# A cross-attention kernel on one core: a new hand-written order for the last ten tiles, and two weight splits moved in the head

## The chip, the cores and the metric

The kernel runs on one core of one Trainium2 chip. The metric is the device time of one execution in microseconds (us). Before the change the median of three runs is 506.95 us, the lowest 506.29 and the highest 507.17. The profile comes from one execution of its own.

## The reference

Queries come from x, keys and values from a context of 77 rows per batch, sixteen heads of 32; the output gets the residual x and a layer norm:

```python
qs = (q @ wq).reshape(Bq, Lq, H, HD).transpose(0, 2, 1, 3)
ks_ = (k @ wk).reshape(Bq, Lk, H, HD).transpose(0, 2, 1, 3)
vs = (v @ wv).reshape(Bq, Lk, H, HD).transpose(0, 2, 1, 3)
scores = jnp.einsum('bhqd,bhkd->bhqk', qs, ks_) / jnp.sqrt(jnp.float32(HD))
scores = jnp.where(mask[:, None, :, :], -jnp.inf, scores)
attn_w = jax.nn.softmax(scores, axis=-1)
attn = jnp.einsum('bhqk,bhkd->bhqd', attn_w, vs)
out = attn.transpose(0, 2, 1, 3).reshape(Bq, Lq, H * HD) @ wo + q
mu = jnp.mean(out, axis=-1, keepdims=True)
var = jnp.mean((out - mu) ** 2, axis=-1, keepdims=True)
return (out - mu) / jnp.sqrt(var + EPS) * gamma + beta
```

x is 4 x 2048 x 512 in fp32, the context 4 x 77 x 512 (both k and v), the mask 4 x 2048 x 77.

## The kernel before, in words

The 8192 rows of x are cut into 64 tiles of 128 rows, taken in 32 pairs; four tiles are a group of the query projection. The projections split each fp32 operand into a high and a low part and sum three products, so the query of a group (L192) and the output projection of a tile (L561) are twelve matmuls of 128x512 each per quarter or tile.

A tile goes through these steps. TensorE makes the scores (L321). VectorE takes each head's maximum and applies the mask (L364), ScalarE the exponential with its sum (L379), VectorE the reciprocal of the sums (L385), GpSimd the normalisation (L390), VectorE a transposition in 32x32 blocks into a buffer B (L413). For each pair of tiles twelve DMAs of 128 KB, the regroups (L425), put the blocks of B into a buffer PT with the keys on the partitions. TensorE multiplies PT with the values vsb (L459). ScalarE writes the high part of the result (L508), VectorE the low part (L512), and TensorE makes the output projection (L561). VectorE adds the rows of x, which a DMA of 256 KB has brought into an output buffer o (load L529, residual L564), and takes the statistics (L599, L606). The reciprocal root is GpSimd's (L638 or L634, then L639), the scaling ScalarE's (L585 or L648) or VectorE's (centre L669, finish L684), the affine step GpSimd's (L589, L590), and a DMA of 256 KB stores the tile (L593). There are eight buffers o; the last tiles use four `o_end` and four `o_last`, in space that other buffers leave.

The last tile, 63, is computed in other ways to finish sooner. Its probabilities are turned by TensorE and not by DMA (L439, L449), and its product needs the values with their rows in another order: `turn_values` (L615, L616) copies 19 and 58 rows of vsb, 2 KB each, into a spare buffer by two DMAs of SyncE. Tile 62 is finished in halves (L679 on ScalarE, L680 on GpSimd, L681), tile 63 by L664 and L674 on VectorE.

The order is written out by hand, and each engine runs its instructions in the order in which the program issues them. A head loop does tiles 0 to 5. A table PAIR of words is read once for each of the pairs 3 to 26. Then JOINT and ORDER, a table for the last ten tiles, are read once, word by word (`for word in (JOINT + ORDER).split(): do(*read(word))`, after L870). A word is a letter and a tile, pair or group piece, with a part behind the point:

- S scores, T maxima of four heads, e exponentials, r reciprocal, n normalisation, t transposition (tiles)
- P regroup of a pair, U regroup of one tile, V product with the values (pairs); a and b are the high and low part of its result, c and d the same for a tile
- O output projection, x load of x, + residual, s statistics, u reciprocal root, v bias, k scaling, p scaling on GpSimd, f affine step, y centre, z finish, B half a finish, w store
- Q query projection of a quarter group, q its evacuation, i and j the high and low part of x transposed
- R, E, X, W, h, m, I, J, M: the special steps of tiles 63 and others; Y0 is turn_values

A letter at the end of a P or U names the engine whose queue issues the DMA: s SyncE, g GpSimd, a ScalarE. Loads and stores are always issued by SyncE. A DMA that must wait (for a transposition, for a buffer that is to be emptied) holds all that stand behind it in its engine's list. The DMAs of SyncE signal on eight semaphores in rotation, so each also waits for the landing of the one eight places before it.

In the head loop, for u = 2, `split_wo` (L289) makes the low part of two of the four rows of the output weights on GpSimd, and `split_xT` (L180) the low part of x transposed.

Of the kernel before, what the change touches and what calls it, by code (L numbers as in the profile page):

```python
# [53 lines left out]
ORDER = """
S54 T54.3 i31 e54.3 T54.0 O49 q58 e54.0 k47 T54.2 T54.1 +49 t53 S55 T55.0 T55.1 Q59 f47 x50 x52 T55.3 e54.2 T55.2
e54.1 j31 r54 n54 O48 q59 s49 P26.9s +48 S56 e55.0 P26.4s e55.2 e55.1 e55.3 T56.1 T56.0 P26.6g P26.0s V25 T56.2 x51
r55 a25.0 a25.1 t54 e56.1 S57 e56.2 T56.3 T57.2 Q62 P26.2g P26.8s n55 e56.3 T57.1 Q60 t55 u49 b25.0 e56.0 P26.3g Q63
e57.1 p49 e57.2 T57.3 T57.0 r56 w47 s48 b25.1 P26.5s x59 e57.3 x53 S58 P26.10s P26.7g P27.7g q62 e57.0 k46 n56 q60
P27.0s q63 u48 p48 T58.1 T58.2 P26.1s P27.1s P26.11s T58.3 e58.1 r57 t56 P27.11s n57 Q61 P27.6s f46 e58.2 T58.0 V26
q61 a26.1 t57 a26.0 x55 f48 e58.0 S59 P27.2s T59.2 P27.5s e58.3 T59.3 e59.3 P27.3s P28.4g P27.8s T59.0 O51 b26.0  # L60
P28.11g T59.1 P27.9s +51 P28.6g r58 e59.2 P28.5g O50 P27.10s b26.1 s51 e59.1 P27.4s n58 S60 Y0 u51 +50 P28.0s x57
e59.0 P28.7g P28.10s V27 T60.0 T60.1 a27.0 T60.2 a27.1 T60.3 e60.1 r59 t58 w46 P28.3s P28.9s S61 n59 O52 P28.1s
e60.3 b27.0 s50 T61.0 T61.3 t59 f49 u50 e61.0 e61.3 T61.2 b27.1 T61.1 O53 P28.8s P29.1g P29.9g e61.2 O54 S62 +52
e61.1 +53 s52 x54 r61 P28.2s V28 +54 P29.7g e60.2 x62 T62.1 T62.2 O55 p50 n61 e60.0 T62.3 x56 P29.4s r60 n60 T62.0
t61 v51 M0 P29.8s a28.0 a28.1 b28.1 b28.0 f50 t60 +55 O57 e62.2 P29.6s e62.1 P29.5s P29.10s +57 P30.6g P29.3s
P29.11s k51 P29.2s P29.0s P30.10s P30.1s e62.0 e62.3 u52 v52 S63 V29 P30.2s T63.0 P30.9s P30.5g s53 P30.7g P30.11a
s55 T63.1 r62 a29.1 P30.4s T63.3 P30.0s e63.0 P30.3s n62 b29.1 T63.2 O56 a29.0 b29.0 e63.1 I54 u53 e63.3 P30.8s s57
h63.0 y55 t62 +56 f51 O59 u55 e63.2 x58 O58 x60 k52 m63.0 y54 V30 h63.1 m63.1 I56 U62.7s U62.6s +59 J56 a30.1 u56
U62.4s U62.8s R63.0 U62.9s x61 U62.11s s59 y57 a30.0 u57 +58 u59 b30.1 b30.0 U62.5s z57 R63.1 y53 J54 R63.3 U62.1s
U62.0a R63.2 w48 E63.0a f52 w51 s58 U62.10s O60 U62.3s y58 +60 w50 O61 U62.2a w52 X63 M1 z53 E63.1a v56 v59 s60 z55  # L70
+61 y60 E63.2a u54 W62 u58 k56 E63.3a w49 w57 u60 z54 k59 I61 c62 w54 J61 W63 f56 z58 c63 d62 y61 w53 z60 w55 u61
f59 O62 w56 d63 z61 +62 s62 y62 w58 w60 w61 w59 O63 u62 s63.0 s63.1 B62.0 u63 B62.1 y63 z63 w63
"""


# [1 line left out]
def xattn_layernorm(  # L77
# [100 lines left out]
    def split_xT(g, c):  # L178
        h, l = (a[:, c : c + 2] for a in gx[g])
        nc.gpsimd.tensor_tensor(l, fx[g, c], h.bitcast(F32), ALU.subtract)  # L180
# [107 lines left out]
    def split_wo(c):  # L288
        nc.gpsimd.tensor_tensor(wol[:, c], stage_b[:, 1, c], woh[:, c].bitcast(F32), ALU.subtract)  # L289
# [93 lines left out]
    def recip(t):  # L383
        ris[t] = sb.tile([P, H], F32, tag="ri", bufs=3, name=f"ri_{t}")
        nc.vector.reciprocal(ris[t], sums[t])  # L385
# [641 lines left out]
```

## Time and profile before

| what | value |
|---|---|
| median of 3 runs | 506.95 us (506.29 to 507.17) |
| the profiled execution | 506.36 us |
| its span, first to last instruction | 504.5 us |
| PE, DVE, ACT, POOL busy | 496.3, 462.7, 473.3, 428.2 us |
| regroups issued by SyncE, by GpSimd in the span | 355, 16 |

The profile is of one execution. PE is TensorE's matmuls and PEld its weight loads, which overlap; DVE is VectorE, ACT ScalarE, POOL GpSimd, SP SyncE. Busy times are sums over instructions of an engine that do not overlap in the sum. An arrow like `PT<-B` names what is written and read; `x12` counts. The queue rows (`SPq`) show when an engine issued a DMA and how long the issue took, not the transfer. Between the time of an execution and its span lie 1.86 us here. The chain of waits follows back from the last instruction what released each step. The table ORDER covers the time from about 414 us on.

### The profile page before, as it was taken

The numbers are of one execution on the slowest core, as the hardware profiler recorded it, in microseconds if no ns is written. First come the engines' busy times: TensorE is split into PE (matmuls) and PEld (weight loads), VectorE is DVE, ScalarE is ACT, GpSimd is POOL, SyncE is SP. The second block draws the span as 40 slices with busy tenths as digits, with TensorE's granted clock in tenths as the row PEclk, the third lists the DMA queues.
The fourth block names the chain that finished last, engine by engine and source line by source line (L and its number), as shares of the span: only waits on it lengthen the run. The fifth ranks groups of instructions, "written<-read, shape, count | busy, mean of one in ns | idle before, by whom it ended". The sixth has DMA issues, their size and how long they took to land.

```text
span 504.5 us, 20435 instructions
## 1 busy us (share of the span) xinstructions
PE 496.3 (98%) x6904; PEld 390.5 (77%) x6904; DVE 462.7 (92%) x2567; ACT 473.3 (94%) x2241; POOL 428.2 (85%) x385
## 2 busy tenths in 40 slices
PE   9999999999999999999999999999999999999995
PEld 7987778877777887777788777778877777777774
DVE  6698999999989988999999988999998889999997
ACT  6798999999999999999999999999999999999871
POOL 0659368989988998998999888899999888999996
PEclk9999999999999999999999999999999999999999
DMA  8945977677777789777778868978787888667665
GB/s 312 400 161 142 220 199 203 201 201 203 214 226 221 210 216 231 217 214 224 217 218 219 241 173 221 253 208 234 220 208 185 236 233 241 167 187 220 168 210 209
DMA packets 58424, 109.50 MB, mean 217 GB/s; under 512 B 9219, under 2 KB 11011, under 8 KB 58320
## 3 DMA queue, kind: packets, MB, share of 16 engines
q1 hardware_dynamic: 55920, 103.35, 72.6%
q0 software_dynamic: 1872, 4.20, 2.8%
q8 instruction: 55, 0.90, 0.8%
q10 hardware_dynamic: 528, 0.66, 0.4%
q14 instruction: 49, 0.40, 0.2%
HBM read 41.68 MB, written 16.78 MB: 116 GB/s over the span
## 4 chain that ended last, share of the span: by engine, by line
PE 82%; DVE 8%; ACT 5%; DMA 1%; POOL 1%; issue 1%; SPq 1%; DVEq 0%; POOLq 0%; ACTq 0%
PE pq L192 28%; PE po L561 26%; PE pa L459 10%; PE sc L321 6%; ACT pbuf L379 4%; PE sc L561 2%; PE sc_e L321 2%; DVE pbuf L364 2%; DVE B L413 2%; PE pv L258 2%; PE pk L218 1%; PE pq L729 1%; PE pq L190 1%; PE sc_f L321 1%; DVE AL L512 1%
## 5 line engine op out<-in xcount | busy, mean ns | idle before, releaser
L379 ACT ACTIVATE pbuf<-pbuf,nm 128x77 f32<-128x77 f32 x1024 | 352.5, 348 | 8.2 <-DVE nm L364 7.5
L379 ACT ACTIVATION_READ_ACCUMULATOR pbuf<-pbuf,nm 128x1 f32 x1024 | 193.1, 189 | 0.0
L390 POOL TENSOR_TENSOR pbuf<-pbuf,ri 128x1232 f32<-128x1232 f32 x63 | 145.8, 2316 | 19.8 <-DVE ri L385 11.8
L364 DVE CUSTOM_DVE_ANT_0 pbuf<-sc,mb 128x77 f32<-128x77 f32 x828 | 143.8, 231 | 5.9 <-PE sc L321 5.6
L192 PE MATMUL pq<-xtl,wqh 128*128 128x512 f32 (+1 forms) x256 | 98.3, 384 | 0.0
L192 PE MATMUL pq<-xth,wql 128*128 128x512 f32 (+1 forms) x256 | 98.2, 384 | 0.0
L413 DVE STREAM_TRANSPOSE B<-pbuf 128x1280 f32<-128x1280 f32 x63 | 94.6, 1502 | 0.5 <-POOL pbuf L390 0.2
L561 PE MATMUL po<-woh,AH 128*128 128x512 f32 x224 | 90.5, 404 | 0.0
L192 PE MATMUL pq<-xth,wqh 128*128 128x512 f32 (+1 forms) x230 | 88.6, 385 | 0.0
L561 PE MATMUL po<-wol,AH 128*128 128x512 f32 x224 | 87.3, 390 | 0.0
L561 PE MATMUL po<-woh,AL 128*128 128x512 f32 x224 | 86.5, 390 | 0.0
L589 POOL TENSOR_TENSOR o<-o,gam 128x512 f32<-128x512 f32 x53 | 68.7, 1297 | 20.8 <-ACT o L585 20.8
L364 DVE DVE_READ_ACCUMULATOR2_ANT nm<- 128x1 f32 x1024 | 84.2, 82 | 0.0
L590 POOL TENSOR_TENSOR o<-o,bet 128x512 f32<-128x512 f32 x53 | 68.4, 1291 | 4.2
L180 POOL TENSOR_TENSOR xtl<-xtf,xth 128x1024 fp32r<-128x1024 f32 x28 | 67.4, 2409 | 0.1
L459 PE MATMUL pa<-PT,vsb 96*32 96x256 f32 x960 | 58.2, 382 | 0.7 <-DVE ri L385 0.3
L321 PE MATMUL sc<-kct,q 32*64 32x77 f32 x3312 | 55.5, 239 | 0.4 <-DVE q L209 0.3
L192 PEld LDWEIGHTS pq<-xth,wql 128*128 128x128 f32 x256 | 48.2, 188 | 8.4
L192 PEld LDWEIGHTS pq<-xtl,wqh 128*128 128x128 f32 x256 | 48.1, 188 | 8.5
L321 PEld LDWEIGHTS sc<-kct,q 32*64 32x64 f32 x3312 | 48.8, 130 | 6.5 <-issue 5.1
L561 PEld LDWEIGHTS po<-woh,AH 128*128 128x128 f32 x224 | 42.0, 187 | 10.7 <-DVE nm L364 0.4
L192 PEld LDWEIGHTS pq<-xth,wqh 128*128 128x128 f32 x230 | 43.2, 188 | 8.9
(195 smaller groups left out, 852.8 us busy)
## 6 DMA issues: line engine op xcount, KB each, us to landing
PT<-B SPq DMA_DIRECT2D x355, 128.0 KB
xtf<-xT SPq DMA_DIRECT2D x28, 512.0 KB
o<-x SPq DMA_DIRECT2D x56, 256.0 KB
out<-o SPq DMA_DIRECT2D x56, 256.0 KB
PT<-B POOLq DMA_DIRECT2D x16, 128.0 KB, 4.4
xtf<-xT SPq DMA_DIRECT2D x4, 256.0 KB
stage_a<-wk SPq DMA_DIRECT2D x4, 256.0 KB
stage_b<-wv SPq DMA_DIRECT2D x4, 256.0 KB
```

The source lines that it names most:

```text
L180: nc.gpsimd.tensor_tensor(l, fx[g, c], h.bitcast(F32), ALU.subtract)
L192: nc.tensor.matmul(pq, wc, r[:, c, rs], start=(n == 0), stop=(n == 11))
L258: nc.tensor.matmul(pv, ctx_s[c][i][:, r, :], v[c], start=(n == 0), stop=(n == 11))
L321: nc.tensor.matmul(scs[t][g, j][r0 : r0 + n], qd[t // 4][q, g, at : at + n], kct[q, g, t // TPB, keys_of(j)], start=True, stop=True,)
L364: nc.vector.tensor_tensor_reduce(pb[:, i // 2, (i % 2) * NK : (i % 2 + 1) * NK], scs[t][g, j], mb[:, t % TPB, keys_of(h)], -1.0, CEIL, ALU ...
L379: nc.scalar.activation(p, p, AF.Exp, bias=nmax[t][:, i : i + 1], scale=-1.0, accum_out=sums[t][:, i : i + 1])
L390: nc.gpsimd.tensor_tensor(pv, pv, rv.to_broadcast((P, NP, 2, NK)), ALU.mult)
L413: nc.vector.transpose(bt.rearrange("p c q r -> p q c r"), pbuf[t % NPB].rearrange("p q (c r) -> p q c r", c=5),)
L459: nc.tensor.matmul(pas[b, g // 2][HD * j : HD * (j + 1), (g % 2) * BLK : (g % 2 + 1) * BLK], vsb[:, 2 * b // TPB, HD * h : HD * (h + 1)], ...
L561: nc.tensor.matmul(pos[t], a[:, c, rs], w[:, c], start=(first and n == 0), stop=(n == 11))
L589: nc.gpsimd.tensor_tensor(o, o, gam, ALU.mult)
L590: nc.gpsimd.tensor_tensor(o, o, bet, ALU.add)
```

## The change

Three edits. First, ORDER is replaced by a new order of the same words, for all engines; only the queues of the regroups differ: 16 were issued by GpSimd and are 8 now, 3 by ScalarE and are 2, and SyncE issues the other nine. Among the order's changes, the product V26 stands ahead of the scores S60 (before, ahead of S59), V25 ahead of S56 (before, behind it) and V28 ahead of S62 (before, behind it). Second, in the head loop at u = 2 the two `split_wo` go behind the two `split_xT`. Third, two unused entries come into the table of operations, which shift the lines behind L831 by one.

```diff
@@ ORDER (first and last lines of each)
-S54 T54.3 i31 e54.3 T54.0 O49 q58 e54.0 k47 T54.2 T54.1 +49 t53 S55 T55.0 T55.1 Q59 f47 x50 x52 T55.3 e54.2 T55.2
...
-f59 O62 w56 d63 z61 +62 s62 y62 w58 w60 w61 w59 O63 u62 s63.0 s63.1 B62.0 u63 B62.1 y63 z63 w63
+k47 i31 f47 j31 k46 S54 T54.0 e54.0 T54.2 e54.2 T54.3 q58 T54.1 O48 +48 t53 P26.9s P26.7s P26.2g P26.3s P26.1s P26.5s
...
+w52 w59 w61 w54 s62 O63 s63.0 y62 u62 B62.1 B62.0 s63.1 u63 y63 z63
@@ -785,8 +785,6 @@
         if u == 2:
             recip(1)
             normalise(1)
-            split_wo(0)
-            split_wo(1)
         for q in evac:
             q_evac(*q)
@@ -795,6 +793,9 @@
         for q in pieces(u):
             split_xT(*q)
+        if u == 2:
+            split_wo(0)
+            split_wo(1)
         if u == 0:
@@ -889,7 +890,7 @@
-        "v": bias_one, "K": stretch, "G": shift, "p": pool_scale, "I": act_mean, "J": act_squares, "M": keep,
+        "A": scores_pair, "D": scores_rest, "v": bias_one, "K": stretch, "G": shift, "p": pool_scale, "I": act_mean, "J": act_squares, "M": keep,
```

SyncE, at the head of the table, before the change (o_7713 is the load x50, o_7715 x52, o_7845 x51; PT_7755 belongs to pair 26 and out<-o_7226 is w47):

```order
L593 DMA out<-o_6928 128x512
L529 DMA o_7713<-x 128x512
L529 DMA o_7715<-x 128x512
L425 DMA PT_7755<-B_7559 32x2x512 x3
L529 DMA o_7845<-x 128x512
L425 DMA PT_7755<-B_7559 32x2x512
L593 DMA out<-o_7226 128x512
```

and, further on, before the change around turn_values (PT_8044 belongs to pair 27, PT_8198 to pair 28, out<-o_7197 is w46):

```order
L529 DMA o_8133<-x 128x512
L425 DMA PT_8044<-B_7853 32x2x512 x7
L615 DMA spare<-vsb 19x512
L616 DMA spare<-vsb 58x512
L425 DMA PT_8198<-B_8080 32x2x512
L529 DMA o_end<-x 128x512
L425 DMA PT_8198<-B_8080 32x2x512
L593 DMA out<-o_7197 128x512
```

The same place of SyncE after the change (PT_7974 is pair 27's, PT_8261 pair 28's; o_8164 is x51, o_8265 x54, o_8268 x50):

```order
L425 DMA PT_7974<-B_7873 32x2x512 x2
L529 DMA o_8164<-x 128x512
L593 DMA out<-o_7226 128x512
L615 DMA spare<-vsb 19x512
L616 DMA spare<-vsb 58x512
L425 DMA PT_7974<-B_7873 32x2x512 x4
L425 DMA PT_8261<-B_8065 32x2x512 x2
L529 DMA o_8265<-x 128x512
L425 DMA PT_8261<-B_8065 32x2x512
L529 DMA o_8268<-x 128x512
L425 DMA PT_8261<-B_8065 32x2x512 x3
```

The loads x50 and x52 have left the head of the table; turn_values stands ahead of four regroups of pair 27 and of x50, which is the eleventh DMA counted from L615.

SyncE after the change, around x52 (o_8626; PT_8462 is pair 29's, out<-o_7469 is w48, out<-o_7197 w46):

```order
L425 DMA PT_8462<-B_8289 32x2x512 x7
L593 DMA out<-o_7469 128x512
L425 DMA PT_8462<-B_8289 32x2x512
L593 DMA out<-o_7197 128x512
L425 DMA PT_8462<-B_8289 32x2x512
L529 DMA o_8626<-x 128x512
```

x52 now follows the regroups of pair 29, and it takes the buffer that w48 stores.

GpSimd's last instructions before the change (mvt_9043 is tile 62's statistics, mvt_9080 tile 63's):

```order
L638 TENSOR_TENSOR mvt_9043<-mvt_9043,small 128x1
L639 TENSOR_TENSOR mvt_9043<-mvt_9043,small 128x1
L680 TENSOR_TENSOR o_last<-o_last,bet 128x256
L639 TENSOR_TENSOR mvt_9080<-mvt_9080,small 128x1
L680 TENSOR_TENSOR o_last<-o_last,bet 128x256
```

and after it (mvt_9054 is tile 62's, mvt_9093 tile 63's):

```order
L589 TENSOR_TENSOR o_end<-o_end,gam 128x512
L590 TENSOR_TENSOR o_end<-o_end,bet 128x512
L638 TENSOR_TENSOR mvt_9054<-mvt_9054,small 128x1
L639 TENSOR_TENSOR mvt_9054<-mvt_9054,small 128x1
L680 TENSOR_TENSOR o_last<-o_last,bet 128x256 x2
L639 TENSOR_TENSOR mvt_9093<-mvt_9093,small 128x1
```

Tile 63's reciprocal root (the last L639) stood between the two halves of tile 62 and stands behind both.

More of the change, by code (lines that the diff above doesn't have):

```diff
@@ L54 @@
 ORDER = """
-S54 T54.3 i31 e54.3 T54.0 O49 q58 e54.0 k47 T54.2 T54.1 +49 t53 S55 T55.0 T55.1 Q59 f47 x50 x52 T55.3 e54.2 T55.2
[L56 to L69, printed above, removed]
@@ L70 @@
-U62.0a R63.2 w48 E63.0a f52 w51 s58 U62.10s O60 U62.3s y58 +60 w50 O61 U62.2a w52 X63 M1 z53 E63.1a v56 v59 s60 z55
-+61 y60 E63.2a u54 W62 u58 k56 E63.3a w49 w57 u60 z54 k59 I61 c62 w54 J61 W63 f56 z58 c63 d62 y61 w53 z60 w55 u61
-f59 O62 w56 d63 z61 +62 s62 y62 w58 w60 w61 w59 O63 u62 s63.0 s63.1 B62.0 u63 B62.1 y63 z63 w63
+k47 i31 f47 j31 k46 S54 T54.0 e54.0 T54.2 e54.2 T54.3 q58 T54.1 O48 +48 t53 P26.9s P26.7s P26.2g P26.3s P26.1s P26.5s
+P26.4s P26.11s Q59 s48 u48 q59 S55 T55.1 V25 e54.1 e54.3 a25.0 e55.1 T55.0 r54 e55.0 T55.2 T55.3 e55.3 e55.2 a25.1 S56
@@ new lines @@
+T56.1 T56.2 b25.0 T56.0 T56.3 e56.3 e56.1 e56.0 e56.2 n54 O49 +49 t54 P26.6s r55 Q60 S57 s49 T57.0 T57.3 T57.1 e57.0
+e57.1 Q61 q60 n55 P26.10g P26.0s p48 t55 P27.7s P26.8s S58 r56 T57.2 e57.3 e57.2 P27.11s P27.1s P27.2g u49 n56 p49
+b25.1 T58.1 T58.3 T58.2 e58.1 T58.0 e58.0 e58.2 t56 q61 Q62 Q63 r57 q62 S59 T59.0 T59.1 O51 x62 P27.4s P27.6s x60
+P27.5s P27.9s x51 w47 Y0 P27.10s P27.0s P27.3s V26 e58.3 e59.0 T59.3 T59.2 e59.3 q63 S60 n57 t57 P27.8s f48 +51 r58
+n58 f49 P28.4s P28.8s P28.7g x54 P28.9s x50 P28.3s P28.2s P28.1s T60.0 T60.2 T60.3 T60.1 t58 O50 a26.1 b26.1 e59.2
@@ new lines @@
+e59.1 +50 V27 a27.0 a27.1 b27.0 r59 n59 f46 e60.0 S61 T61.0 T61.1 e61.1 b27.1 T61.3 O54 s51 +54 O55 u51 a26.0 e61.3
+T61.2 e61.2 e61.0 s50 t59 x59 P28.6s P29.1g x55 P28.5s +55 x57 P28.10s P29.8g P28.11s x58 P28.0s x53 P29.4s P29.0s
+P29.2s u50 P29.9g P29.6s P29.5s P29.3s V28 S62 r61 b26.0 a28.0 a28.1 b28.1 b28.0 T62.1 T62.0 s55 T62.3 O57 n61 t61
+e60.1 e60.2 e60.3 r60 v51 p50 O52 +57 T62.2 s57 P29.10s w48 P29.11s w46 P29.7s x52 +52 n60 t60 x56 P30.6s P30.8s
+P30.7s P30.10s P30.9s P30.0s P30.11s x61 P30.5s f50 w50 O56 +56 S63 T63.3 e62.1 e62.0 e62.3 e62.2 r62 T63.1 T63.0 u55
@@ new lines @@
+n62 V29 k51 s52 M0 I54 y54 a29.1 b29.1 I56 a29.0 b29.0 t62 J56 e63.0 P30.4a e63.1 u56 f51 P30.3s u52 O53 +53 h63.0
+m63.0 v56 v52 P30.2s U62.7a e63.3 U62.6s P30.1s U62.4s U62.5s U62.1s U62.3s U62.2s U62.8g U62.9s U62.0s T63.2 e63.2
+O58 +58 y55 O59 s58 y57 V30 a30.1 a30.0 h63.1 m63.1 R63.0 R63.3 M1 E63.3a E63.0a R63.2 E63.2a J54 +59 s53 y58 u58 u53
+s59 b30.0 b30.1 O60 u57 z57 u59 v59 u54 k56 f56 y53 z58 +60 z55 s60 z54 y60 O61 +61 u60 z60 z53 k59 k52 f52 w57
+U62.11s X63 R63.1 U62.10s W62 E63.1a W63 c62 I61 d62 J61 c63 y61 d63 u61 f59 O62 +62 z61 w58 w49 w56 w60 w51 w55 w53
```

## The prediction

> **What bounds the kernel now.** I read the page's busy shares first, then its chain of waits.
>
> ```profile
> PE 496.3 (98%) x6904; PEld 390.5 (77%) x6904; DVE 462.7 (92%) x2567; ACT 473.3 (94%) x2241; POOL 428.2 (85%) x385
> PE 82%; DVE 8%; ACT 5%; DMA 1%; POOL 1%; issue 1%; SPq 1%; DVEq 0%; POOLq 0%; ACTq 0%
> ```
>
> TensorE is busy 98% of the span and carries 82% of the chain. Over the kernel it is the limit, and an order cannot shorten its work. But the change lies in the last ten tiles, so I asked for the stretch that the new table covers, from the first maximum of tile 54 to the last instruction of VectorE (columns: length, then busy time of PE, PEld, DVE, ACT and POOL with instruction counts, the granted clock, the DMA share and GB/s).
>
> ```profile
> 414.81:501.21 86.40, 82.75 (x1119) 64.46 (x1117) 84.35 (x424) 74.71 (x361) 80.61 (x92) 1.00 0.70 203
> DVE AL L512 <- ACT AH L508: 1.6, 3, 1.0
> DVE ri L385 <- ACT pbuf L379: 0.2, 1, 0.2
> DVE B L413 <- POOL pbuf L390: 0.2, 1, 0.2
> ```
>
> Here VectorE is the busiest: 84.35 of 86.40 us, so it idles 2.05 us, and it ends last. The three lines are all of its waits from 412 on (total, times, longest). It waited 0.2 us for GpSimd, and never for a load. So the tail's time is VectorE's work, which the change conserves (the same words stand in both tables), plus its waits. A gain is at most about 2.05 us. A loss has no such bound.
>
> **Prices on VectorE.** These rows of its timeline give start-to-start times.
>
> ```profile
> 414.81 0.23 DVE L364 CUSTOM_DVE_ANT_0 pbuf<-sc,mb 128x77 f32<-128x77 f32 x1
> 416.07 0.69 DVE L209 COPY q<-pq 128x512 f32<-128x512 f32 x1
> 416.67 0.23 DVE L364 CUSTOM_DVE_ANT_0 pbuf<-sc,mb 128x77 f32<-128x77 f32 x1
> 430.69 1.51 DVE L413 STREAM_TRANSPOSE B<-pbuf 128x1280 f32<-128x1280 f32 x1
> 432.12 0.65 DVE L512 TENSOR_TENSOR AL<-pa,AH 128x512 fp32r<-128x512 f32 x1
> 433.95 0.25 DVE L385 RECIPROCAL ri<-sum 128x16 f32<-128x16 f32 x1
> 434.12 0.64 DVE L599 BATCH_NORM_STATS2 st<-o 128x6 f32<-128x512 f32 x1
> 434.89 0.66 DVE L512 TENSOR_TENSOR AL<-pa,AH 128x512 fp32r<-128x512 f32 x1
> ```
>
> From 414.81 to 416.07 stand eight heads, so a T (four heads) is 0.63. A q is 0.60 (416.67 − 416.07), a t 1.43 (432.12 − 430.69), an r 0.17, an s 0.77, and b and + are one pass over 128x512 like q, 0.60 to 0.66.
>
> **The split of the output weights** (head loop). The trace has these rows on GpSimd.
>
> ```profile
> 36.13 2.56 POOL L289 TENSOR_TENSOR wol<-stage_b,woh 128x512 fp32r<-128x512 f32 x2
> 38.63 4.76 POOL L180 TENSOR_TENSOR xtl<-xtf,xth 128x1024 fp32r<-128x1024 f32 x2
> 43.35 2.25 POOL L390 TENSOR_TENSOR pbuf<-pbuf,ri 128x1232 f32<-128x1232 f32 x1
> ```
>
> The two blocks change places: 2.56 + 4.76 is 7.32 either way, so the normalisation behind them still starts at 43.35. The inputs' low parts come 2.5 us sooner, the weights' 4.7 us later, and TensorE has no wait there that either would end: 0, with bounds of −0.2 and +0.2.
>
> **The early part of the table.** The queries, scores and products of tiles 54 to 57 change places on TensorE. I count two new short waits on VectorE (the maxima of tile 57 behind S57, and the transpose of tile 56 behind its normalisation), each at the size of the two 0.2 waits above: 0.45, bounds 0 and 1. GpSimd issues eight fewer regroup DMAs, but VectorE's whole wait for GpSimd is 0.2 us; that is all that can come back by it, and it is in the 2.05.
>
> **The load of x for tile 50.** Before, SyncE issues it at the head of the table; the row holds x50 and x52.
>
> ```profile
> 417.85 1.08 SPq L529 DMA_DIRECT2D o<-x  x2
> 440.44 1.88 SPq L425 DMA_DIRECT2D PT<-B  x3
> 423.90 3.24 DMA PT<-B
> 447.88 3.84 DMA out<-o
> PT<-B POOLq DMA_DIRECT2D x5, 128.0 KB, 5.7
> ```
>
> A regroup issue is 0.63 (1.88 / 3). A 128 KB regroup landed after 3.24 us, a 256 KB store after 3.84; a load of x moves 256 KB too. In the new order x50 is the fifth DMA from P28.4, which must wait for the transpose of tile 57 (t57). Work of VectorE from 414.81 to the end of t57: 24 T, 6 q, 5 t, 4 r, and 2 each of +, s and b, 30.6 us, with the 0.45 so at 445.9. Its residual +50, which reads the load, stands 5.3 us later (one +, r, T x4, t and b), at 451.2. By count alone x50 goes at 445.9 + 4 × 0.63 = 448.4 and lands at 451.6 to 452.2: 0.4 to 1.0 late.
>
> But ahead of these, in the new order, SyncE issues the two loads of turn_values (Y0), 19 and 58 rows of the values. Before, they went at 442.85, and all of tile pair 27's regroups had gone by then.
>
> ```profile
> 442.85 0.72 SPq L615 DMA_DIRECT2D spare<-vsb  x1
> 443.62 0.66 SPq L616 DMA_DIRECT2D spare<-vsb  x1
> 444.52 0.67 SPq L425 DMA_DIRECT2D PT<-B  x1
> 445.87 1.90 SPq L425 DMA_DIRECT2D PT<-B  x1
> 448.46 2.28 SPq L425 DMA_DIRECT2D PT<-B  x2
> 450.78 1.45 SPq L425 DMA_DIRECT2D PT<-B  x1
> 452.28 1.65 SPq L425 DMA_DIRECT2D PT<-B  x1
> 442.00:443.00 1.00, 1.00 (x65) 0.89 (x54) 1.00 (x2) 1.00 (x4) 1.00 (x1) 1.00 0.89 211
> 444.00:445.00 1.00, 1.00 (x6) 0.84 (x5) 1.00 (x15) 1.00 (x7) 1.00 (x2) 1.00 0.08 16
> 445.00:446.00 1.00, 1.00 (x7) 0.81 (x6) 1.00 (x9) 1.00 (x7) 0.92 (x2) 1.00 0.12 33
> 448.00:449.00 1.00, 1.00 (x60) 0.66 (x63) 0.96 (x4) 1.00 (x7) 1.00 (x3) 1.00 0.86 244
> 449.40 0.85 PE L459 MATMUL pa<-PT,vsb 96*32 96x256 f32 x12
> ```
>
> Behind them the mean DMA share falls from 0.89 to 0.08 and 0.12, one and two of sixteen engines, and is back at 448, although a regroup was issued at 444.52: it stood behind the two. [...] Counting from L615 as the first, the ninth went at 450.78 (+7.9 us) and the tenth at 452.28 (+9.4).
>
> [...]
>
> Now SyncE reaches Y0 so: it is held at P27.7 by the transpose t55, which ends after 19.4 us of VectorE's work (15 T, 3 q, 3 t and seven short ones), so at 434.6 with the 0.45, and twelve issues of 0.63 follow: 442.1. Behind Y0 stand four regroups of pair 27 that the product V27 needs, and x50 is the eleventh from it. By the distances above it goes at +8.0 (if it goes as soon as the ninth did) to +11.1 (9.4 + 1.65): 450.1 to 453.2, and lands 3.24 to 3.84 later, at 453.3 to 457.0. VectorE waits 2.1 to 5.8 us at +50. I take 3.5, nearer the lower end: the same ten microseconds of before also had five regroups of GpSimd's queue (the row with POOLq above) on the engines, where the new order has two. V27's wait for its four regroups (they move when traffic does, near 447.5, plus 3.24, so at 450.7 or later, against TensorE's arrival at 449.4, the start of V27 in before: the same products stand ahead of it in both orders) lies under that wait: 0 for itself, up to 1 if not.
>
> **The load of x for tile 52.** From t59 to +52 VectorE has 8.9 us of work (2 +, 2 r, 3 b, 4 T, 2 s, 1 t). SyncE issues twelve DMAs from the end of t59: seven regroups, the store w48, one regroup, w46, one regroup, x52. x52 takes the buffer that w48 empties: w48 goes at 7 × 0.63 = 4.4 and lands 3.24 to 3.84 later, at 7.6 to 8.2; x52 lands at 10.9 to 12.1. The wait is 2.0 to 3.2; as before SyncE's pace varies by an issue or two, 1.3 to 3.2. I take 1.9, since the DMA engines are less loaded there. In before it was issued with x50, near 418.
>
> **Pairs 28 and 30.** P28.0 now goes after fifteen others, and U62.6 (it waits for t62) stands ahead of P30.1, which V30 needs. VectorE's work covers both within an issue or so: 0.2 each, bounds 0 and 1.8.
>
> **The end.** Rows of before, in the order of the dependence:
>
> ```profile
> 497.59 0.75 DVE L669 SCALAR_TENSOR_TENSOR o_last<-o_last,mvt,row 128x512 f32<-128x512 f32 x1
> 498.49 0.91 ACT L679 ACTIVATE o_last<-o_last,mvt 128x256 f32<-128x256 f32 x2 [5.20 <-POOL mvt L639]
> 499.07 0.72 POOL L680 TENSOR_TENSOR o_last<-o_last,bet 128x256 f32<-128x256 f32 x1 [0.62 <-ACT o_last L679]
> 499.75 0.55 POOL L639 TENSOR_TENSOR mvt<-mvt,small 128x1 f32<-128x1 f32 x1
> 500.34 0.87 DVE L674 SCALAR_TENSOR_TENSOR o_last<-o_last,mvt,pa 128x256 f32<-128x256 f32 x2
> ```
>
> The last finish (z63) needs the reciprocal root L639 of tile 63, which stood between the two additions L680; now it stands behind both. From y62 (L669) to VectorE's end it was 3.62 us. Now: 0.90 to L679, 0.58 to L680, two additions of 0.72, 0.55 and 0.87, 4.34 us, and y62 stands behind one half of tile 63's statistics. VectorE's own work from y62 on is 0.7 + 0.7 + 0.9 + 0.9 = 3.1, so it waits 1.2 (bounds 0.7 and 1.3).
>
> **The sum.** 0.45 + 3.5 + 1.9 + 0.2 + 0.2 + 1.2 − 2.05 (all of before's waits, given back) = +5.4 us. The profiled execution, 506.36 (span 504.5 and 1.86 around it), becomes 511.8; the median of the three runs is 506.95, so 512.4.
>
> **The rivals.**
>
> 1. Y0 does not hold the queue for x50. For it: in before nobody waited on it. Against it: the shares of 0.08 and 0.12. Then +50 waits 0.8 and not 3.5: 506.95 + 2.7 = 509.6, slower still by x52 and the end. [...]
>
> 2. The other side: the loads are in time. If the order lets SyncE run ahead (P28.4 and P29.4 not held, Y0 over sooner), x50 lands before 451.2 and x52 within 8.9 us of t59; the early waits vanish with GpSimd's eight issues gone. Then only the end's 0.7 is left against 2.05: −1.3, 505.6. It decides at 451.2: every microsecond that x50 lands later costs one. Between this and rival 1, one load is late by about 1.5 us and the sum is nothing.
>
> 3. The waits add up instead of covering each other: V27 and pair 28, each up to 1 to 1.8, make ScalarE late with the exponentials behind them, or x50 lands at 457: 506.95 + 5.4 + 2.8 = about 515.2.
>
> 4. The new table changes nothing in the waits and the swap in the head is all that acts: 0. The order of SyncE above speaks against it.
>
> **How the numbers follow.** A measurement of this kernel can tell about 0.2%, 1.0 us, from no change. Forecast 0.60, rival 1 0.17, rival 3 0.06 (all slower); rival 2 0.11; rival 4 and the sum of nothing 0.06. So slower 0.83, same 0.06, faster 0.11. The range reaches from 508.0 (rival 1 with x52 only 0.4 late) to 515.2 (rival 3); what it leaves out is rival 2, the same and a tail of rival 3.
>
> **What would show it.** Right: in the new trace VectorE's L564 of tile 50 sits idle 2 to 6 us near 451 and of tile 52 1 to 3 us near 470, both ended by a load; the DMA share falls to about 0.1 for some 3 us from 443; L639 stands behind two L680 at the end. Wrong: L564 without idle time; Y0 issued later than 444 or the share above 0.5 behind it (rival 1); a wait of TensorE or ScalarE that is longer than VectorE's; or a head that moves by more than 0.2 us.

## The result, and the profile after

The changed kernel takes 519.12 us (median of six runs, 517.13 to 521.92) against 506.71 us for the kernel before (six runs, 506.29 to 507.17): ratio 1.0248, 95% interval 1.0218 to 1.0278, 12.4 us slower. The prediction said 512.4 with a range to 515.2: the right side, and less than half of the loss. The profiled execution took 519.87 us with a span of 518.0.

The page's busy shares after:

```profile
PE 501.7 (97%) x6904; PEld 393.7 (76%) x6904; DVE 462.7 (89%) x2567; ACT 474.2 (92%) x2241; POOL 423.9 (82%) x377
```

The stretch of the table, from the first maximum of tile 54 to VectorE's last instruction (length, then the busy time of PE, PEld, DVE, ACT and POOL with counts, the granted clock, the DMA share and GB/s):

```profile
415.38:515.15 99.77, 87.79 (x1119) 67.09 (x1117) 84.50 (x424) 75.67 (x361) 76.07 (x84) 0.94 0.63 178
```

Ten microseconds of it, in the kernel before:

```profile
450.00:460.00 10.00, 10.00 (x126) 7.94 (x116) 9.97 (x67) 10.00 (x57) 9.42 (x12) 1.00 0.87 256
```

and in the changed one:

```profile
450.00:460.00 10.00, 7.61 (x104) 4.81 (x104) 5.99 (x29) 5.93 (x31) 6.53 (x6) 0.66 0.87 248
```

VectorE's work in the stretch is what it was, 84.50 us against 84.35. Its idle time has gone from 2.05 to 99.77 − 84.50 = 15.27 us. That difference, 13.2 us, is nearly the whole loss of this execution (13.5 us of span; the tail began 0.57 us later, and the span ended 0.44 us sooner after VectorE). TensorE is busy 5.0 us longer over the same instructions, and the column of the granted clock shows why: 0.66 in these ten microseconds, where it was 1.00. Nothing in the prediction spoke of the clock.

VectorE's waits in the changed kernel from 410 on (total, times, longest) are these:

```profile
DVE AL L512 <- ACT AH L508: 4.3, 4, 2.7
DVE o L564 <- DMA o<-x: 3.8, 2, 3.6
DVE B L413 <- POOL o L590: 2.5, 1, 2.5
DVE pbuf L364 <- PE sc L321: 1.7, 2, 1.4
DVE o_last L564 <- PE sc L561: 1.1, 2, 0.8
DVE o_last L674 <- POOL mvt L639: 1.0, 1, 1.0
```

And this is where the longer ones stand on VectorE's timeline (the idle time before the row, and what ended it, in brackets):

```profile
452.44 1.51 DVE L413 STREAM_TRANSPOSE B<-pbuf 128x1280 f32<-128x1280 f32 x1 [2.45 <-POOL o L590]
454.71 0.69 DVE L564 TENSOR_TENSOR o<-po,o 128x512 f32<-128x512 f32 x1 [0.18 <-DMA o<-x]
457.55 0.24 DVE L364 CUSTOM_DVE_ANT_0 pbuf<-sc,mb 128x77 f32<-128x77 f32 x1 [1.39 <-PE sc L321]
477.87 0.69 DVE L564 TENSOR_TENSOR o<-po,o 128x512 f32<-128x512 f32 x1 [3.64 <-DMA o<-x]
496.26 1.29 DVE L512 TENSOR_TENSOR AL<-sc,AH 128x512 fp32r<-128x512 f32 x2 [2.71 <-ACT AH L508]
514.28 0.87 DVE L674 SCALAR_TENSOR_TENSOR o_last<-o_last,mvt,po 128x256 f32<-128x256 f32 x2 [1.03 <-POOL mvt L639]
```

and of TensorE:

```profile
452.57 3.64 PE L459 MATMUL pa<-PT,vsb 96*32 96x256 f32 x32 [2.39 <-DMA PT<-B]
480.61 0.50 PE L561 MATMUL po<-woh,AH 128*128 128x512 f32 x1 [2.10 <-DVE o_end L564]
492.46 2.65 PE L459 MATMUL sc<-PT,vsb 96*32 96x256 f32 x32 [3.27 <-DMA PT<-B]
```

Read from the top. At 452.44 the transpose of tile 58 starts after 2.45 us of idle time. The profile names GpSimd, but GpSimd's normalisation of that tile had ended 2.6 us before: by the landings in the trace the last regroup of pair 27 came in at 452.22, and the transpose writes the buffer B that those regroups read (two buffers B are in turn, pair 29's is pair 27's). At the same time, at 452.57, V27 starts on TensorE, 2.39 us late, and takes 3.64 us, where it took 1.93 in the kernel before. The residual of tile 50 then waits only 0.18 us. The residual of tile 52 waits 3.64 us; V30 waits 3.27 us and VectorE 2.71 behind it. The last finish waits 1.03.

The DMA share behind turn_values, whose two copies went at 443.29 and 444.07, did not fall as it had in the kernel before (0.08 and 0.12 there):

```profile
444.00:445.00 1.00, 1.00 (x15) 0.48 (x17) 1.00 (x11) 1.00 (x7) 1.00 (x2) 1.00 0.92 301
445.00:446.00 1.00, 1.00 (x28) 0.53 (x19) 1.00 (x2) 1.00 (x7) 0.92 (x2) 1.00 0.34 115
446.00:447.00 1.00, 1.00 (x70) 0.71 (x64) 1.00 (x2) 1.00 (x7) 0.64 (x1) 1.00 0.78 96
447.00:448.00 1.00, 1.00 (x30) 0.78 (x12) 1.00 (x9) 1.00 (x7) 0.41 (x1) 1.00 0.72 129
```

It stood above 0.5 in two of the three microseconds from 445 on, which the prediction had named as a sign of rival 1. What fell is the rate, from 301 to between 96 and 129 GB/s, and what shows the hold are the landings: the four regroups of pair 27 issued behind the copies landed 5.4 to 6.4 us after their issue.

### The profile page after: what moved, and what is told of

The parts are those of the page before. It is cut to its first block, busy times and chain, and to the rows that moved or that the text cites. A ratio compares the mean times of both kernels' runs of the same rounds, so it can differ in the third digit from the quotient of the medians.

```text
span 518.0 us, 20437 instructions
## 1 busy us (share of the span) xinstructions
PE 501.7 (97%) x6904; PEld 393.7 (76%) x6904; DVE 462.7 (89%) x2567; ACT 474.2 (92%) x2241; POOL 423.9 (82%) x377
## 4 chain that ended last, share of the span: by engine, by line
PE 88%; DMA 3%; DVE 3%; SPq 2%; POOL 1%; issue 1%; POOLq 0%; ACT 0%; DVEq 0%; ACTq 0%
PE pq L192 30%; PE po L561 29%; PE pa L459 10%; PE sc L321 7%; SPq L425 2%; PE sc_e L321 2%; PE pv L258 2%; PE sc L561 2%; PE pk L218 1%; DMA PT<-B 1%; PE pq L729 1%; PE pq L190 1%; PE sc_f L321 1%; DVE pbuf L364 1%; DMA o_last<-x 1%
## 5 line engine op out<-in xcount | busy, mean ns | idle before, releaser
L561 PE MATMUL po<-woh,AH 128*128 128x512 f32 x232 | 94.6, 408 | 2.1 <-DVE o_end L564 2.1
L561 PE MATMUL po<-wol,AH 128*128 128x512 f32 x232 | 90.9, 392 | 0.0
L561 PE MATMUL po<-woh,AL 128*128 128x512 f32 x232 | 88.6, 390 | 0.0
L459 PE MATMUL pa<-PT,vsb 96*32 96x256 f32 x960 | 59.7, 390 | 3.0 <-DMA PT<-B 2.4
L561 PEld LDWEIGHTS po<-woh,AH 128*128 128x128 f32 x232 | 43.9, 189 | 13.5 <-DVE o_end L564 2.6
L459 PEld LDWEIGHTS pa<-PT,vsb 96*32 96x32 f32 x960 | 29.3, 111 | 28.9 <-issue 10.2
```

The costliest lines, as they stand in the source:

```text
L459: nc.tensor.matmul(pas[b, g // 2][HD * j : HD * (j + 1), (g % 2) * BLK : (g % 2 + 1) * BLK], vsb[:, 2 * b // TPB, HD * h : HD * (h + 1)], ...
L561: nc.tensor.matmul(pos[t], a[:, c, rs], w[:, c], start=(first and n == 0), stop=(n == 11))
```

## The experiments

Measured beside the runs, the kernel before took 506.66 to 506.97 us (medians). Each run's ratio to it is given with its 95% interval; the changed kernel has 1.0248 [1.0218, 1.0278]. The diffs show the main places of an edit; "..." stands for what lies between them.

**turn_values moved out of the way** (e1). Behind x53 SyncE waits anyway.

```diff
-P27.5s P27.9s x51 w47 Y0 P27.10s P27.0s P27.3s
+P27.5s P27.9s x51 w47 P27.10s P27.0s P27.3s
...
-x53 P29.4s P29.0s
+x53 Y0 P29.4s P29.0s
```

> The changed kernel with one move: turn_values (Y0) goes behind the load x53, where SyncE waits anyway, so the four regroups of pair 27 and x50 no longer stand behind it. Theory A (late regroups of pair 27 hold V27 and, through the buffer B, the transpose of tile 58; TensorE's wait of 2.4 us there is followed by a granted clock of 0.5 for 6.8 us): the waits of 2.45 us (tile 58) and 2.39 us (V27) and the half clock behind them vanish, 519.1 becomes 513 to 515.5. Theory B (only the held queue counts, the clock plays no part): 2.6 us less, 516.5. If the regroups of pair 27 are late by themselves: 519.

Measured: 516.5 us, ratio 1.0192 [1.0171, 1.0214], 2.6 us less. The waits at V27 and at tile 58 are gone, x50 is 1.26 us late, and now V28 waits, with VectorE behind it:

```profile
453.33 0.69 DVE L564 TENSOR_TENSOR o<-po,o 128x512 f32<-128x512 f32 x1 [1.26 <-DMA o<-x]
464.11 3.64 PE L459 MATMUL pa<-PT,vsb 96*32 96x256 f32 x32 [3.99 <-DMA o<-x]
468.42 1.29 DVE L512 TENSOR_TENSOR AL<-pa,AH 128x512 fp32r<-128x512 f32 x2 [5.66 <-ACT AH L508]
```

The first waits were turn_values' doing, as both theories said. The time is theory B's, but not for its reason: the clock stayed at 1.00 behind V27 and fell behind V28 (3.64 us for the product, the time of V27's at 0.50 in the changed kernel), whose regroups became the wait.

**x52 early** (e2) and **x50 early** (e4), each an exchange of two words.

```diff
-x53 P29.4s P29.0s
+x52 P29.4s P29.0s
...
-P29.7s x52 +52
+P29.7s x53 +52
```

> The changed kernel with the loads x52 and x53 exchanged on SyncE, so x52 goes some 13 us earlier and x53, whose residual comes later, takes its place. Theory A: the wait of 3.64 us at the residual of tile 52 vanishes, the transpose of tile 60 behind it and the twelve regroups of pair 30 come earlier by as much, TensorE's wait of 3.27 us at V30 shrinks and with it the half clock that follows it: 512.5 to 515. Theory B (that wait alone): 515.5. If V30 waits for tile 62's transposition instead: 517 to 519.

Measured: 517.59 us, 1.0215 [1.02, 1.023]: perhaps 1.5 us less, where 4 to 6.5 were expected. The wait at tile 52 went, and V28 waited 1.63 us and V30 2.79 us instead.

```diff
-x62 P27.4s P27.6s x60
+x62 P27.4s P27.6s x50
...
-P28.9s x50 P28.3s
+P28.9s x60 P28.3s
```

> The changed kernel with the loads x50 and x60 exchanged on SyncE, so x50 goes ahead of turn_values. The term of the prediction (x50's lateness is what VectorE waits for, 3.5 us): 515.5. Theory A (the wait has gone to the transpose of tile 58, which needs pair 27's regroups; 0.18 us is left at the residual of tile 50): 518.8 to 519.2.

Measured: 520.11 us, 1.0267 [1.0231, 1.0304], no different from the changed kernel, as theory A said (a little above its 519.2). The wait at tile 58 grew to 3.90 us and the one at tile 52 was 2.52. The time of the term that carried the prediction's sum, 3.5 us at the residual of tile 50, cannot be won by loading tile 50 sooner: another wait stands in the same place.

**A wait filled with work** (e3).

```diff
-        for n, (_, c, a, w) in enumerate(prods):
-            nc.tensor.matmul(pos[t], a[:, c, rs], w[:, c], start=(first and n == 0), stop=(n == 11))
+        for again in range(2 if t == 50 else 1):
+            for n, (_, c, a, w) in enumerate(prods):
+                nc.tensor.matmul(pos[t], a[:, c, rs], w[:, c], start=(first and n == 0), stop=(n == 11))
```

> The changed kernel with twelve matmuls more: the output projection of tile 50 is done twice into the same bank (the second pass replaces the first), 2.72 us of TensorE's work put just where it waits 2.39 us for V27's regroups. Theory A (the wait itself brings the granted clock down): with the wait filled the clock stays at 1.0 around 452 to 459, V27 takes 1.9 and not 3.6 us, and the kernel gets faster by 1 to 2.5 us though it does more: 516.5 to 518. Theory B (the clock's drop isn't caused by the wait, or doesn't matter): the same to 0.5 us slower, 519 to 519.6.

Measured: 518.7 us, 1.0245 [1.0212, 1.0279]: no difference that can be told, so theory A's gain of 1 to 2.5 us did not come. The clock stayed at 1.00 from 450 to 460 and fell one stage later, behind a wait of 3.04 us at V28:

```profile
450.00:460.00 10.00, 7.71 (x117) 5.29 (x117) 5.61 (x27) 5.06 (x25) 4.81 (x4) 1.00 0.93 226
466.00:474.00 8.00, 7.70 (x105) 5.03 (x106) 3.35 (x21) 4.59 (x23) 6.30 (x8) 0.57 0.91 257
```

and that wait on TensorE's timeline:

```profile
466.30 3.64 PE L459 MATMUL pa<-PT,vsb 96*32 96x256 f32 x32 [3.04 <-DMA o<-x]
```

The half clock followed the wait, but its price stayed open, so it was tried again in a kernel with one wait only, below.

**The queues alone, in the kernel before** (e5, e10, e11). At their old words, regroups change from GpSimd to SyncE: one of pair 26, four of pair 28, three of pair 30; then pair 28's alone, then pair 30's.

```diff
-P28.4g ... P28.11g ... P28.6g ... P28.5g
+P28.4s ... P28.11s ... P28.6s ... P28.5s
...
-P30.6g ... P30.5g ... P30.7g
+P30.6s ... P30.5s ... P30.7s
```

> The kernel before with one thing of the change alone: eight regroups that GpSimd issued (one of pair 26, four of pair 28, three of pair 30) are issued by SyncE, at the same words. Theory C (SyncE's list sets the tail: from a pair's last transposition to its product SyncE has twelve regroups less those of GpSimd and whatever else stands there, 0.63 us each): V28 and V30 get 1.9 to 2.5 us less room, the kernel goes from 507.0 to 508.5 to 511. Theory D (the loss lies in the new order of the computing engines; the queues are a side matter): 506.5 to 507.5.

> The kernel before with only the four regroups of pair 28 on SyncE's queue, at their words, which stand among those of pair 27. If they are what costs in the run with all eight (they wait for the transposition of tile 57 and hold pair 27's regroups, turn_values and the loads behind them): 513 to 517. If every regroup costs alike: 507.0 and half of 10.5, 512. If pair 30's are what costs: 507 to 508.

> The kernel before with only the three regroups of pair 30 on SyncE's queue, at their words. If pair 28's are what costs: 507 to 508.5 (three issues more, 1.9 us, ahead of V30). If pair 30's are: 512 to 517.

Measured: all eight 517.44 us, 1.0203 [1.0174, 1.0232]; pair 28's 511.09, 1.0083 [1.0059, 1.0108]; pair 30's 515.35, 1.0164 [1.0147, 1.0181]. The first is far above what either theory said, pair 28's lies nearest to the forecast by which each regroup costs alike (512), and pair 30's is in the range named for it. Pair 30's three regroups cost twice what pair 28's four do, and the two parts add up to more than the whole. With nothing else changed, these letters cost what most of the change costs. The run with pair 30's shows how: on SyncE, one row covers the regroups of pairs 29 and 30, and V29 waits 5.49 us. The row hides a pause: seen from 463 on, its issues begin at 469.47 (the second line).

```profile
458.04 22.38 SPq L425 DMA_DIRECT2D PT<-B  x20
469.47 10.95 SPq L425 DMA_DIRECT2D PT<-B  x15
```

In the kernel before, four regroups went in that pause:

```profile
462.11 2.51 SPq L425 DMA_DIRECT2D PT<-B  x4
```

and TensorE's wait for it:

```profile
476.15 1.93 PE L459 MATMUL pa<-PT,vsb 96*32 96x256 f32 x16 [5.49 <-DMA PT<-B]
```

P30.6 stands among pair 29's last regroups and must wait for the transposition of tile 60, which ended at 469.39. In the kernel before, GpSimd came to it at 470.05, when that transposition was over, and it held no other regroup; on SyncE's queue it holds P29.3, .11, .2 and .0, the four that went at 462.11 before, and V29 with them. So in these three runs it is less the 0.63 us of an issue that counts than what stands behind a DMA that cannot go yet. In the changed kernel the words were moved too, so this price is not simply the change's.

**The price of the half clock** (e14). The run with pair 30's regroups on SyncE has one long wait. 24 matmuls of no use fill it.

```diff
             pas[b, i] = bank(f"pa_{b}_{i}")
+        if b == 29:
+            for n in range(24):
+                nc.tensor.matmul(pas[b, 0], at[28][0][:, 0, :P], woh[:, 0], start=True, stop=True)
```

> The kernel before with pair 30's three regroups on SyncE, and 24 matmuls more on TensorE ahead of V29: they multiply what is there (the high parts of pair 28 and of the weights) into the bank that V29 then overwrites, 5.4 us that fill its wait of 5.5 us. If the granted clock of 0.5 for 10.2 us is brought about by that wait: the clock stays at 1.0, V29 ends no later, and the kernel is faster by 1.5 to 5 us: 510.5 to 514. If the clock falls for another reason: 515 to 516.

Measured: 512.94 us, 1.0118 [1.0103, 1.0134], against 1.0164 [1.0147, 1.0181] without them: 2.4 us faster with 24 matmuls more. From 474 to 484, without them:

```profile
474.00:484.00 10.00, 7.85 (x43) 5.00 (x44) 3.28 (x20) 4.11 (x19) 6.01 (x7) 0.52 0.85 210
```

and with them:

```profile
474.00:484.00 10.00, 10.00 (x68) 7.40 (x68) 4.87 (x17) 6.01 (x30) 6.96 (x8) 1.00 0.80 198
```

The clock is 1.00 where it was 0.52. In this kernel TensorE's wait of 5.49 us brings the clock down, and the slow work behind it is a price of its own.

**Six regroups back on GpSimd** (e6), with pair 30's three behind the affine step of tile 50.

```diff
-P28.4s P28.8s P28.7g x54 P28.9s
+P28.4g P28.8g P28.7g x54 P28.9g
...
-f50 w50 O56
+f50 P30.3g P30.2g P30.1g w50 O56
```

> The changed kernel with six regroups given back to GpSimd: three of pair 28 at their words, three of pair 30 put behind the affine step of tile 50. Theory C: V30's wait (3.3 us, with a half clock behind it) goes, the waits at V27 and at the residual of tile 52 stay: 515 to 517. Theory D: 518.5 or more, GpSimd's own work being later by 3.5 us.

Measured: 517.35 us, 1.0211 [1.0171, 1.0252], close above what theory C said, and at the edge of what can be told from the changed kernel. V30's wait fell to 0.95 us; V27 (2.62) and V28 (2.04) still waited, each with a half clock behind it (V28's product took 3.33 us, where V27's took 1.93 in the kernel before).

**Only the DMAs in another order** (e7, e8, e9, e13). The work of TensorE, ScalarE, VectorE and GpSimd stays as in the change, but for the end's few words in e8, e9 and e13. The six regroups given back to GpSimd in the run before stay there.

```diff
-P26.0s p48 t55
+P26.0s x50 x51 x54 x55 w47 x52 x62 x60 p48 t55
...
-P27.5s P27.9s x51 w47 Y0 P27.10s P27.0s P27.3s
+P27.5s P27.9s P27.10s P27.0s P27.3s P27.8s
...
-P28.0s x53 P29.4s
+P28.0s x59 x57 x58 w48 x53 Y0 P29.4s
```

> The changed kernel with the order of the four computing engines' own work untouched and the DMAs alone put in another order: the six regroups as in the run on GpSimd's queue; the loads of tiles 50, 51, 54, 55, 52, 62 and 60 and the store 47 ahead of pair 27's regroups, in SyncE's idle time; the other loads, the store 48 and turn_values behind pair 28's regroups; U62.6, x61, w46 and w50 behind the regroups of their place. Theory C: nearly all waits of VectorE and TensorE go, and the half clocks with them: 505.5 to 508.5. Theory D: 511 or more.

Measured: 517.05 us, 1.0203 [1.0169, 1.0238]. Theory C failed in this form: the transpose of tile 56 waited 4.99 us (P26.8, which it needs, stood behind the early loads) and the residual of tile 56 3.58 us (its load was last). The run with the end's order mended as well:

```diff
-s62 O63 s63.0 y62 u62 B62.1 B62.0 s63.1 u63 y63 z63
+s62 O63 s63.0 y62 u62 s63.1 B62.1 u63 B62.0 y63 z63
```

> The same with tile 63's reciprocal root between the two halves of tile 62's finish, as before the change, and the second half of tile 63's statistics ahead of them. The prediction's term for the end (1.2 us of wait, of which 1.03 was seen): 0.7 to 1.1 us less than the run with the DMA order alone. If the end hangs on something else (TensorE's last products): the same within 0.3.

Measured: 515.97 us, 1.0167 [1.0137, 1.0197]. The last finish waited 0.34 us and not 1.03, so 0.7 of the end's term is shown. The rest of the difference cannot be the edit's, which stands later in the program: in the two profiled executions the transpose of tile 56 waited 4.99 and 3.32 us, and a half clock behind V29 came in the first (a mean of 0.57 from 479 to 483) and not in the second. Then P26.8 ahead, and x52 and x56 behind pair 27's regroups:

```diff
-P26.0s x50 x51 x54 x55 w47 x52 x62 x60 p48
+P26.0s P26.8s w47 x50 x51 x54 x55 x62 x60 p48
...
-P28.0s x59 x57 x58 w48 x53 Y0 P29.4s
+P28.0s Y0 x59 x57 x58 w48 x53 P29.4s
```

> The changed kernel with its DMAs alone in a third order (and tile 63's root between the halves of tile 62, as in the run before): P26.8 stays ahead of the early loads, so the transpose of tile 56 isn't held; x56 and x52 go behind pair 27's regroups, turn_values right behind pair 28's, and w46 behind pair 30's. The work of TensorE, ScalarE and VectorE stands as in the change. Theory C (the loss lies in the DMAs' order and queues, the order of the computing engines is neutral): 506 to 509. Theory D (the computing order itself leaves the regroups too little time): 511 or more, with waits of TensorE at V28, V29 or V30 that are left.

Measured: 513.78 us, 1.0162 [1.0115, 1.0208]; three of four runs within 0.3 us of 513.7. By the time it is theory D's case, though of V28, V29 and V30 only V28 still waited; turn_values' move did not end that:

```profile
462.02 3.64 PE L459 MATMUL pa<-PT,vsb 96*32 96x256 f32 x32 [3.82 <-DMA PT<-B]
```

By the landings in the trace three regroups that GpSimd issued at 452.5 to 453.6, while SyncE issued the second part of turn_values (landed 459.68), came in 7.6 to 8.1 us later. So turn_values holds regroups of another queue as well.

```diff
-P27.8s x52 x56
+P27.8s Y0 x52 x56
```

> The run with the third order of the DMAs and one move more: turn_values goes from behind pair 28's regroups to behind the last one of pair 27, ahead of the loads x52 and x56. Theory C: GpSimd's regroups of pair 28 no longer stand behind it on the DMA engines, V28's wait of 3.8 us, VectorE's 5.55 us behind it and the half clock of 6.8 us go: 506 to 508.5. Theory D (the new computing order leaves too little time somewhere): another wait of 2 us or more takes its place, 510 or more.

Measured: 513.0 us, 1.0113 [1.0092, 1.0134], theory D's side again. V28 still waited 2.94 us: now all of pair 28 stood behind turn_values and landed 5 to 8.3 us after its issue.

**turn_values in four copies** (e15, e16), in the changed kernel and in the run just told.

```diff
-        nc.sync.dma_start(v[:TAIL_K], vsb[NK:, NB - 1])
-        nc.sync.dma_start(v[TAIL_K:NK], vsb[: NK - TAIL_K, NB - 1])
+        for lo, hi in ((0, 16), (16, 19), (19, 67), (67, 77)):
+            at0 = NK + lo if lo < TAIL_K else lo - TAIL_K
+            nc.sync.dma_start(v[lo:hi], vsb[at0 : at0 + hi - lo, NB - 1])
```

> The changed kernel with turn_values as four copies of 16, 3, 48 and 10 rows at the same place, and not two of 19 and 58. If the two held the queue because they run on one and two of the sixteen DMA engines, the DMAs behind them land 2.5 to 4 us after their issue, the waits of 2.4 us at the transpose of tile 58 and at V27 shrink and the half clock behind V27 goes: 515 to 517.5. If what holds there is SyncE's issue rate: 518.5 to 519.5 (two issues more).

Measured: 520.98 us, 1.0278 [1.0258, 1.0297], above both forecasts and not faster. But the hold is shown: the regroups behind it landed 2.3 to 2.5 us after their issue (4.5 to 6.4 in the changed kernel), V27 waited 0.46 us and the transpose of tile 58 0.50. What came instead has the place and the size of the prediction's own term, but not its cause, as nothing was held: x50 went at 450.94 (451.60 in the changed kernel) and landed 4.87 us later (3.01 there); why it took so long was not tested.

```profile
450.05 1.51 DVE L413 STREAM_TRANSPOSE B<-pbuf 128x1280 f32<-128x1280 f32 x1 [0.50 <-DMA PT<-B]
455.91 0.69 DVE L564 TENSOR_TENSOR o<-po,o 128x512 f32<-128x512 f32 x1 [3.77 <-DMA o<-x]
456.74 0.47 PE L561 MATMUL po<-woh,AH 128*128 128x512 f32 x1 [3.65 <-DVE o L564]
```

> The run with the DMAs in order and turn_values behind pair 27's regroups, with the same four copies. If the held engines are all that is left: V28's wait of 2.9 us, VectorE's 3.6 us and the half clock go, 513.0 becomes 506.5 to 509.5. If the new computing order leaves pair 28 too little room (11.7 us from the transposition of tile 57 to V28, twelve regroups and the landing take 11): 510 to 512.

Measured: 511.02 us, 1.0073 [1.005, 1.0096], the fastest with the new computing order, and still 4.1 us slower than before. The time is the one named for too little room at pair 28, but that is not what the trace shows: V28 waits 0.39 us. The longest waits left are for GpSimd, which has the regroups back and no idle time from 464 to 483:

```profile
485.84 0.94 PE L439 MATMUL pa<-ident,pbuf 128*77 128x128 f32 x4 [2.20 <-POOL pbuf L403]
488.17 0.75 DVE L685 SCALAR_TENSOR_TENSOR o_end<-o_end,mvt,po 128x512 f32<-128x512 f32 x1 [1.72 <-POOL mvt L640]
```

**GpSimd's list** (e17): U62.8 behind tile 63's second normalisation, the affine step of tile 51 behind the reciprocal root of tile 54.

```diff
-u56 f51 u52
+u56 u52
...
-U62.8g U62.4s
+U62.4s
...
-m63.1 R63.0
+m63.1 U62.8g R63.0
...
-u54 k56
+u54 f51 k56
```

> The run with the DMAs in order and turn_values in four copies, and two moves on GpSimd: the regroup U62.8 goes behind the second normalisation of tile 63, and the affine step of tile 51 behind the reciprocal root of tile 54. If GpSimd's list is what is left: TensorE's wait of 2.2 us falls to 1 or less, the half clock behind it goes, and VectorE's waits of 1.72 and 1.14 us with them: 507.5 to 509.5. If the new order of TensorE and VectorE leaves them waiting anyway: 510.5 to 511.5.

Measured: 512.05 us, 1.0111 [1.0093, 1.0128]. Both forecasts missed. TensorE's wait at tile 63 went, and VectorE waited 2.17 us for another reciprocal root of GpSimd's. Whether the new computing order could be as fast as the old one with a still better list stays open.

**The head alone** (e12), in the kernel before.

```diff
-            split_wo(0)
-            split_wo(1)
         for q in evac:
...
             split_xT(*q)
+        if u == 2:
+            split_wo(0)
+            split_wo(1)
```

> The kernel before with only the change in the head: the two splits of the output weights behind the two of x transposed on GpSimd. The prediction's term: 0, so 506.8 to 507.2. A loss in the head would show as a later start of the tail by over 0.5 us.

Measured: 506.74 us, ratio 0.9999 [0.999, 1.0008]. The move of the splits does nothing.

## Why the prediction was wrong

Step by step, by the terms of its sum.

- **The frame** holds: VectorE's work is conserved, the loss is its idle time, 15.27 against 2.05 us. The head is 0, as said. In that idle time the terms measured 0.76 (early waits, 0.45 said), 2.63 (tile 50, 3.5), 3.64 (tile 52, 1.9), 2.71 (pairs 28 and 30, 0.4) and 1.03 (the end, 1.2); another 4.0 us are waits that no term named, and 1.5 were given back (2.05 said).
- **The waits given back**, 2.05: read too high. The three lines of waits count from 412 on and sum to 2.0, near 2.05 by chance. Their places are these:

```profile
413.33 0.69 DVE L512 TENSOR_TENSOR AL<-pa,AH 128x512 fp32r<-128x512 f32 x1 [1.01 <-ACT AH L508]
414.20 0.69 DVE L512 TENSOR_TENSOR AL<-pa,AH 128x512 fp32r<-128x512 f32 x1 [0.17 <-ACT AH L508]
426.98 0.25 DVE L385 RECIPROCAL ri<-sum 128x16 f32<-128x16 f32 x1 [0.22 <-ACT pbuf L379]
464.88 1.51 DVE L413 STREAM_TRANSPOSE B<-pbuf 128x1280 f32<-128x1280 f32 x1 [0.17 <-POOL pbuf L390]
483.35 0.69 DVE L512 TENSOR_TENSOR AL<-pa,AH 128x512 fp32r<-128x512 f32 x1 [0.42 <-ACT AH L508]
```

The first two, 1.18 us, lie ahead of the stretch, and they came in the changed kernel too. In the stretch stand 0.81 us of waits and 1.24 us of gaps of under 0.15 us each. The change gave back the 0.81 and 0.71 of the 1.24.
- **The early waits** were put at 0.45; they are 0.28 and 0.48, at the two places that were named.
- **turn_values and x50**, 3.5 us: that turn_values holds what is issued behind it is shown, by the run that moves it (x50 goes at 449.46) and by the one that makes it four copies (the regroups behind it land after 2.3 to 2.5 us, where the four of pair 27 took 5.4 to 6.4). Y0 went at 443.29 (442.1 was said), x50 at 451.60 (450.1 to 453.2) and landed at 454.61; its residual started at 454.71, when the load was said to land at 454.7. That these two agree is partly luck, since the residual was late itself. For the wait was told at the wrong instruction. The step that failed is "V27's wait for its four regroups ... lies under that wait: 0 for itself". V27 and the transpose of tile 58 waited first, 2.39 and 2.45 us, and left 0.18 for x50; and TensorE's wait was not free though VectorE waited at the same time, because the clock behind it was 0.50 for 6.83 us. I had not followed the buffer B, which makes the transpose of a later tile wait for regroups to land. So loading tile 50 sooner gained nothing, and in the run with the four copies x50 is 3.77 us late without the hold.
- **The half clock** is missing from the sum. Behind V27 TensorE ran at 0.50 for 6.8 us and behind V30 for 3.4 us, which makes 5.1 us of its work late. VectorE's 1.39, 0.45 and 0.48 us between 457 and 467, and 0.77 at 500, stand right behind it, some 3 of the 4.0 us that no term named; that they come from it is argued from their places. In the kernel where its price could be measured by itself, one fall of 10.24 us was worth 2.4 us.
- **x52**, 1.9 us: right in kind, 3.64 in size. The twelve issues took longer than 0.63 each: the seven regroups ahead took 5.99 us and the load landed 12.8 us after t59, where 10.9 to 12.1 had been worked out. I had taken 1.9, below the 2.0 to 3.2 that the rows gave.
- **Pairs 28 and 30**, "0.2 each": the step that failed most. V30 waited 3.27 us and VectorE 2.71. The wait at tile 52 pushed the transposition of tile 60; P30.1, the last regroup that V30 needs, was the fourteenth DMA of SyncE's behind that transposition, issued 9.0 us after its end, at 489.02, and landed at 492.05; and the room that the product leaves its regroups had shrunk. From the end of a pair's last transposition to the moment when TensorE is ready for its product there are 17.2 (pair 27), 18.1 less 0.3 (28), 12.9 (29) and 11.7 us (30) in before; after, 15.1, 17.3 (with 5.8 us of TensorE's waiting and slow work in it), 11.6 and 9.2. Thirteen issues of 0.63 and a landing of 3.24 make 11.4 us, hardly less than the 11.7 of before and more than the 9.2 of after. That subtraction for each product would have named pair 30 as the place to look at. It was never made. That V28 came off with 0.42 us is luck: without the 5.8 us ahead of it, in the run with turn_values moved, it waited 3.99 us.
- **The end**, 1.2 us: 1.03 seen, 0.7 of it undone by the reorder.
- **Rival 3** (the waits add up) is what happened, given 0.06, and its 515.2 was still too low: it had no clock of 0.50 behind V27 and V30.
- **The signs** went both ways. L639 stands behind both L680, and the residual of tile 52 waits for its load. But the residual of tile 50 idles 0.18 us and not 2 to 6, the DMA share did not fall to 0.1, and TensorE's wait at V30 (3.27) is longer than VectorE's behind it (2.71), which had been named as a sign of being wrong.

GpSimd's eight regroups are the part that was dismissed with "VectorE's whole wait for GpSimd is 0.2 us; that is all that can come back by it". In before, they stood on a queue where they held no other pair's regroups. That moving them costs much is shown at their old words (10.5 us, twice the 8 × 0.63 = 5.0 us that their issues take on SyncE), not for the change itself, where giving six of them back gained 1.8 us, hardly more than can be told. The runs in which one wait was taken away show why no single term accounts for it: SyncE's list is late at four places in a row (V27, V28, the residual of tile 52, V30), and each mended place lets TensorE or VectorE run to the next. With the computing order kept, but for the end's few words, another order of the DMAs, six of them back on GpSimd and turn_values in four copies brought 519.1 down to 511.0 us: some 8 of the 12.4 us are shown to lie there. What share of the last 4 us belongs to the new computing order, and what to a list of GpSimd and SyncE that could be better, is not settled.

## What to carry to other kernels

Before an order is costed by what stands on the path, subtract, for each product that needs a set of transfers, the time from the event that frees them to the product, and set it against issues times pace plus a landing, on the queue that carries them (counting the other DMAs that stand between them); and follow each buffer back to whoever must let go of it. In an in-order queue a DMA that waits costs what stands behind it (on SyncE, P30.6 held four regroups of pair 29, and V29 waited 5.49 us), so the queue that is idle most is worth more than its issue time (10.5 us here, at 5.0 us of issues). When several places are late, expect that mending one moves the wait and does not remove it (with turn_values moved, V27's 2.39 us went and V28 waited 3.99).
